# A graph network layer on one core: 32 instead of 24 columns an octet picked by TensorE, slightly fewer by ScalarE and VectorE, and the remainder table's operations in two places of VectorE's octet

## The chip, the core and the metric

The kernel runs on one core of a Trainium2 chip. The time is device microseconds of that core, the median of three runs. The profile and the trace come from one further execution on the same kind of core.

## The reference

A graph has 12,500 nodes with 64 features and 400,000 edges, sorted by their destination node. Each edge brings 16 features of its own. The layer makes a message for each edge, sums the messages of each node, and updates the nodes:

```python
m_in = jnp.concatenate([x[src], x[dst], edge_attr], axis=-1)
h = jax.nn.silu(m_in @ W1 + b1)
messages = jax.nn.silu(h @ W2 + b2)
agg = jax.ops.segment_sum(messages, dst, num_segments=x.shape[0])
node_in = jnp.concatenate([x, agg], axis=-1)
x = layernorm(x + jax.nn.silu(node_in @ W3 + b3))
```

Everything is float32. What is awkward is `x[src]`: the sources are random, so 400,000 rows of 256 bytes have to be fetched one by one.

## The kernel before, in words

**Tiles and octets.** 128 edges are a tile, and eight tiles are an octet, worked on as four pairs of tiles. There are 391 octets, and the main loop runs over them in order (`o`). Three octets make a chunk, for which the edge features are loaded together.

**Where a source row comes from.** A pair of tiles needs its 256 source rows. The kernel has five ways to get them, and they run side by side on different engines:

- POOL fetches a tile with one indirect DMA (L538, two for a pair) from `pa`, a table of `x @ W1[:64]` that the kernel writes to device memory in the first octets. Buffers for the fetched octets (`ga`) are five; POOL works three octets ahead.
- ScalarE (ACT) keeps `x` transposed in on-chip memory (`xs` in the lower half of the partitions, `x2` in the upper) and copies a column for each edge. One ACTIVATE with a column of `xs` as input and a column of `x2` as bias writes two edges (L447). 128 of them fill the table `cx` of one pair.
- VectorE (DVE) does the same with a maximum of two columns (L449).
- TensorE (PE) picks columns too: a matmul with a fixed matrix and one column of `xs` as moving operand puts the column into a PSUM bank. The first three tables (`EXACT`) are picked in float32 (L396). The later ones take two matmuls for a column, one with the upper 16 bits of `xs` (L400) and one with the remainder table `rest2` (L402). When a table is complete, DVE copies it out of PSUM in four pieces (`place`, L414) into `px`.
- SP fetches single rows with small direct DMAs (`rows`).

An octet's pairs that have a ready table (`slots`) or single rows (`rpairs`) are not gathered by POOL; the rest are. Tables are addressed by node numbers, which the engines read into registers first, 16 or 32 at a time; this is an instruction of the engine's own sequencer (L430 for DVE and ACT, L382 for PE).

**How the work is shared out.** `shares(eng, o)` says how many edges' columns an engine copies in octet `o`: for ACT 80 or 64, for DVE 64 or 96, by the ratio `VRATE`. `filled(o, b)` counts PE's picked columns of PSUM bank `b` ahead of octet `o`, 16 an octet for the exact tables and `PCOLS[1]` an octet after. `rcount` counts the single rows by the ratio `ROWS`. From these counts the lists `pairs`, `slots` and `rpairs` follow: a table is used two octets after it is full.

**One octet on each engine.** The order is written out by hand for PE, ACT, DVE and SP. Ahead of it, POOL runs freely until its `ga` buffers are all in use.

- PE: `turn(o + 1)` transposes the comparison of destinations (L605, into `ph`, one buffer), `window_product(o + 1)` (L562), `first_layer(o)` (L640 for gathered tiles, L643 for tables, L644 for destinations and edge features), the first half of the picks, `add_up(o - 4)` (L671), `second_layer(o - 2)` (L656, L658), the second half of the picks.
- ACT: a block of columns, SiLU of the first layer (`h`, L647), a block of columns, SiLU of the second (`m`, L662).
- DVE: `add_window` (L682), `place` if a table is complete, `compare_nodes(o + 2)` (`eh`, L587), two remainder operations in octets 9 to 58, a block of 16 column copies (for 32 edges), `window_copy(o + 1)` (L567), `turned(o + 1)` (`oh`, L615), a second block, and in some octets a third. Node updates are spread among these.

**The remainder table.** `remainders(k)` makes `rest2`, the part of `x` that the upper 16 bits leave out, 512 columns at a time in four steps: L810 for the lower half of the partitions, L812 (upper half, into spare space `left` of `v`), L814 (a copy of that to `rest2`), L816 (the difference of `left` and `rest2`). 25 blocks of columns make 100 steps. PE first reads `rest2` in octet 58.

Of the kernel before, what the change touches and what calls it, by code (L numbers as in the profile page):

```python
# [32 lines left out]
BEGIN = 4  # L33
PICK = 10
TABLES = 7
ACOLS = (48, 32)
VCOLS = (32, 0, 32, 32)
BASES = 16
PCOLS = (16, 24)
EXACT = 3  # L40
BATCH = 16
ROWS = (220, 13)
VRATE = (18, 7)
LOADS = (16, 32)
AADDR = 15616
RADDR = AADDR + 7360
# [16 lines left out]
def kernel(  # L63
# [51 lines left out]
    with ExitStack() as inner:  # L115
        flag = windows(inner, tc, ident, identb, twice, badi, pa, x, xt, xt2, src_c, src_row, src_pair, dst_c, dst_row, attr_t, attr_2, base, w1, b1, w2, b2, w3, b3, out, edges)
# [5 lines left out]
def windows(ctx, tc, ident, identb, twice, badi, pa, x, xt, xt2, src_c, src_row, src_pair, dst_c, dst_row, attr_t, attr_2, base, w1, b1, w2, b2, w3, b3, out, edges):  # L122
# [5 lines left out]
    NO = base.shape[1]  # L128
# [184 lines left out]
    with tc.tile_pool(name="gat", bufs=AHEAD + 2) as gat, \  # L313
# [20 lines left out]
        def shares(eng, o):  # L334
            if o < BEGIN:
                return (0, 0, 0, 0)
            if eng == ENG.Activation:
                return ACOLS if (o - BEGIN) % 7 % 3 < 2 else (ACOLS[0] - 16, ACOLS[1])
            n = (o + 1 - BEGIN) * VRATE[0] // VRATE[1] - (o - BEGIN) * VRATE[0] // VRATE[1]
            return VCOLS if n == 3 else VCOLS[:3] + (0,)  # L340


        def filled(o, b):
            first = range(PICK + (b - PICK) % 2, len(octs) + 8, 2)
            whole = EXACT * P // PCOLS[0]
            n = len(range(first.start, o, 2))
            return PCOLS[0] * min(n, whole) + PCOLS[1] * max(0, n - whole)

# [4 lines left out]
        for eng in (ENG.Activation, ENG.DVE):  # L353
            counts[eng] = [0]
            for o in range(len(octs) + 8):
                counts[eng].append(counts[eng][-1] + sum(shares(eng, o)))
# [59 lines left out]
        def columns(o, eng, part):  # L416
            if o < BEGIN:
                return
            lo = counts[eng][o] + sum(shares(eng, o)[:part])
            hi, most = lo + shares(eng, o)[part], LOADS[eng == ENG.DVE]  # L420
            while lo < hi:
                j, e0 = lo // (2 * P), lo % (2 * P)
                if j >= len(pairs[eng]):
                    return
                n = min(hi - lo, 2 * P - e0, most)
                key = eng, pairs[eng][j]
                if key not in cols:
                    cols[key] = cx.tile([P, P], F32, name="cx")
                t = cols[key].bitcast(U8)
                _, regs = nc.values_load_multi_w_load_instructions(  # L430
                    indices[eng, j][0:1, e0:e0 + n], engines=(eng,), min_val=XADDR,
                    max_val=X2ADDR + 4 * (N - 1), skip_runtime_bounds_check_because="src names a node")

                def at(i, u, a):
                    return u[:, ds(regs[i].with_bounds(min_val=a, max_val=a + 4 * (N - 1)) - a, 4)]

                def word(i, u, a):
                    o = (regs[i] - a).with_bounds(min_val=0, max_val=4 * (N - 1), guaranteed_mod_val=0, out_of_modulus=4)
                    return u[:, ds(o, 4)].bitcast(F32)

                for i in range(n):
                    e = e0 + i
                    if e % 8 >= 4:
                        continue
                    k = e // 8 * 4 + e % 4
                    if eng == ENG.Activation:
                        nc.scalar.activation(cols[key][:, k:k + 1], word(i, xb, XADDR), AF.Identity, bias=word(i + 4, x2b, X2ADDR))  # L447
                    else:
                        nc.vector.tensor_tensor(t[:, 4 * k:4 * k + 4], at(i, xb, XADDR), at(i + 4, x2b, X2ADDR), op=OP.max)  # L449
                lo += n  # L450
# [4 lines left out]
        def rcount(o):  # L455
            return max(0, o - RAW) * ROWS[0] // ROWS[1]

# [102 lines left out]
        def window_product(o):  # L560
            pw = mis.tile([P, P], F32, name="mm")
            nc.tensor.matmul(pw[:E, :], winrow[o], w1bb.rearrange("k s m -> k (s m)"),  # L562
                             start=True, stop=True)
            winrow[o] = pw

        def window_copy(o):
            nc.vector.tensor_tensor(xw[o % 3][:E, :], winrow.pop(o)[:E, :], mask[:E, :], op=OP.mult)  # L567
# [11 lines left out]
        def compare_nodes(o):  # L579
            c, t0, n, first, last = octs[o]  # L580
            eh = ehp.tile([P, OT // 2, S, 2], F32, name="eh")
            rel = dcs[t0 // SCT].bitcast(F32)
            t0 = t0 % SCT

            def compare(i, k, s, w):
                at = t0 + 2 * i + s
                nc.vector.tensor_tensor(eh[:, i:i + k, :, s:s + w], row[:, None, :, None].to_broadcast([P, k, S, w]),  # L587
                                        rel[:, at:at + k * w].rearrange("p (i s) -> p i s", s=w)[:, :, None, :].to_broadcast([P, k, S, w]),
                                        op=OP.is_equal)

            k = n // 2
            compare(0, k, 0, 2)
            if n % 2:
                compare(k, 1, 0, 1)
                nc.vector.memset(eh[:, k, :, 1], 0.0)
            hots[o] = [eh]
# [12 lines left out]
        def turned(o):  # L609
            c, t0, n, first, last = octs[o]  # L610
            eh, ph = hots[o]
            e = o % 3 * OT // 2 * P
            w = (n + n % 2) // 2 * P
            oh = loaded[c][:, e:e + w]
            nc.vector.tensor_copy(oh[:E, :], ph[:E, :(n + 1) // 2].rearrange("p i e -> p (i e)"))  # L615
            hots[o] = oh, eh
# [155 lines left out]
        for q in range(rest):  # L772
            o = lead[due[q]] + LAST - 1
# [11 lines left out]
        for q0, q1 in batches:  # L785
            o = lead[due[q1 - 1]] + LAST + 2 * G
# [10 lines left out]
        def remainders(k):  # L797

            c = k // 4 * RW
            if c >= N:  # L800
                return
            w = min(RW, N - c)
            at = slice(c, c + w)

            def top(t):
                return t.bitcast(BF16).rearrange("p (n s) -> p n s", s=2)[:, at, 1]

            left = v[D:, 2 * RB - 2:].rearrange("p a i d -> p (a i d)")[:, :w]
            if k % 4 == 0:
                nc.vector.tensor_tensor(rest2[:D, at], xs[:D, at], top(xs)[:D], op=OP.subtract)  # L810
            elif k % 4 == 1:
                nc.vector.tensor_tensor(left, x2[D:, at], top(x2)[D:], op=OP.subtract)  # L812
            elif k % 4 == 2:
                nc.vector.tensor_copy(rest2[D:, at], left)  # L814
            else:
                nc.vector.tensor_tensor(rest2[D:, at], left, rest2[D:, at], op=OP.subtract)  # L816
# [52 lines left out]
        with tc.manual_schedule(engines={ENG.PE, ENG.Activation, ENG.DVE, ENG.SP}):  # L869
# [8 lines left out]
            for o in range(NO + 2):  # L878
# [50 lines left out]
                        nc.vector.memset(t[:, c:min(c + XC, w)], 0.0)  # L929
                if o + 2 < NO:  # L930
                    compare_nodes(o + 2)
                for k in (2 * (o - BEGIN - 5), 2 * (o - BEGIN - 5) + 1) if o >= BEGIN + 5 else ():
                    remainders(k)
                columns(o, ENG.DVE, 0)
                def behind():
                    for q in adds.get(o, []):
# [18 lines left out]
                if o + 1 < NO:  # L955
                    if o + 1 < NO - 1:
                        window_copy(o + 1)
                    if o + 1 == NO - 2:
                        window_product(o + 2)
                        window_copy(o + 2)  # L960
                    columns(o, ENG.DVE, 1)
                    turned(o + 1)
                    columns(o, ENG.DVE, 2)
                columns(o, ENG.DVE, 3)
                if phase == 20:
# [62 lines left out]
def general(ctx, tc, ident, x, xt, src_c, dst_c, dst_row, attr_t, w1, b1, w2, b2, w3, b3, out, edges):  # L1028
# [9 lines left out]
    assert turns * U * P == edges  # L1038
    ROWS = N + P

# [3 lines left out]
    pb = dram.tile([N, D], F32, name="gpb")  # L1044
    accs = [dram.tile([ROWS, D], F32, name=f"acc{k}") for k in range(NACC)]

# [34 lines left out]
    with tc.tile_pool(name="gpre", bufs=3) as pre, tc.tile_pool(name="zero", bufs=1) as zp, \  # L1081
            tc.tile_pool(name="gpre_ps", bufs=4, space=PSUM) as pps:
        width = ROWS * D // P
        assert width * P == ROWS * D
        zero = zp.tile([P, width], F32, name="zero")
# [197 lines left out]
```

## Time and profile before

| what | value |
|---|---|
| median of three runs | 3247.89 us (3245.48 to 3252.06) |
| the profiled execution's own time | 3249.99 us |
| its span, first to last instruction | 3248.0 us |
| mean granted TensorE clock | 0.783 |
| PE busy (matmul) | 2642.2 us, 81% |
| DVE busy | 2119.8 us, 65% |
| ACT busy | 3084.4 us, 95% |
| POOL busy | 2425.1 us, 75% |
| indirect gathers by POOL (L538) | 2459 from `pa`, 84 from `x` |
| column copies by ACT (L447) and DVE (L449) | 14336 and 15616 |
| picks by PE of two matmuls (L400, L402) | 7680 |

A busy share is an average over the run; the octets before 58 differ from those behind it, as PE's picks and the remainder steps do. Idle time marked "issue" is time in which the engine waited for nothing that the profile shows; register loads of its own sequencer are among it.

### The profile page before, as it was taken

How to read it: one execution, taken by the hardware profiler on the slowest of the kernel's cores; microseconds unless marked ns; L12 is line 12 of the kernel's file. 1: busy time of each engine (PE TensorE's matmuls, PEld its weight loads, DVE VectorE, ACT ScalarE, POOL GpSimd, SP SyncE). 2: the span in 40 equal slices, each digit the busy share in tenths (PEclk: the TensorE clock that was granted, in tenths of full speed). 3: DMA queues.
4: the chain of work that ended last, by engine and by line, in shares of the span. 5: the costliest groups of instructions: out<-in, count | busy, mean ns of one | idle time of the engine just before them, and what ended most of it. 6: DMA issues, size and time to landing. Idle time of an engine off the chain costs nothing. (4 is left out here: it accounts for less than half of the span.)

```text
span 3248.0 us, 124643 instructions
## 1 busy us (share of the span) xinstructions
PE 2642.2 (81%) x32267; PEld 2170.6 (67%) x32267; DVE 2119.8 (65%) x18208; ACT 3084.4 (95%) x15185; POOL 2425.1 (75%) x2551
## 2 busy tenths in 40 slices
PE   7788778788787887887888888878888778888776
PEld 5677667676676766666666667667666666666664
DVE  5577777666666666666666666666666666666663
ACT  2799988999999999999999999999999999999994
POOL 7777776777777777777777777777777777777775
PEclk8787877787777777878877777877778788777887
DMA  7211111221221221222221222222221221222211
GB/s 148 49 41 40 40 39 37 43 48 42 43 43 41 49 43 43 43 46 44 43 44 41 46 43 43 43 43 46 43 44 41 45 46 42 44 43 45 44 41 36
DMA packets 157997, 148.42 MB, mean 46 GB/s; under 512 B 101606, under 2 KB 111604, under 8 KB 156516
## 3 DMA queue, kind: packets, MB, share of 16 engines
q0 software_dynamic: 81376, 83.49, 13.5%
q1 hardware_dynamic: 61406, 47.11, 5.6%
q10 hardware_dynamic: 14502, 9.75, 1.4%
q8 instruction: 272, 4.46, 0.6%
q14 instruction: 441, 3.61, 0.4%
HBM read 133.72 MB, written 6.40 MB: 43 GB/s over the span
## 5 line engine op out<-in xcount | busy, mean ns | idle before, releaser
L538 POOL DMA_INDIRECT ga<-pa,sc x2459 | 2344.6, 953 | 772.0 <-issue 661.0
L447 ACT ACTIVATE cx<-xs,x 128x1 f32 x14336 | 2829.6, 412 | 18.8 <-issue 14.8
L449 DVE TENSOR_TENSOR cx<-xs,x 128x4 uint8 x15616 | 1261.1, 155 | 1009.4 <-issue 989.8
L658 PEld LDWEIGHTS p<-w2d,h 128*128 128x128 f32 x3126 | 512.7, 233 | 245.9 <-issue 227.9
L402 PEld LDWEIGHTS <-twice 128*128 128x128 bf16 x7680 | 434.8, 100 | 265.5 <-issue 257.2
L400 PEld LDWEIGHTS <-twice 128*128 128x128 bf16 x7680 | 469.6, 100 | 124.6 <-issue 124.6
L644 PE MATMUL p<-oh,xw 128*128 128x512 f32 x760 | 545.9, 811 | 0.0
L400 PE MATMUL pg<-xs,twice 128*128 x7680 | 478.5, 165 | 69.5 <-DVE px L414 35.6
L658 PE MATMUL p<-w2d,h 128*128 128x128 f32 x3126 | 514.5, 319 | 0.0
L402 PE MATMUL pg<-rest,twice 128*128 x7680 | 468.0, 164 | 1.6 <-DVE rest L816 1.6
L605 PE MATMUL ph<-identb,eh 128*96 128x128 bf16 x1563 | 206.6, 271 | 243.2 <-DVE oh L615 237.2
L656 PE MATMUL p<-b2r,one 128*128 128x512 bf16 x391 | 172.6, 441 | 232.3 <-ACT m L662 231.3
L605 PEld LDWEIGHTS <-eh 128*96 128x96 bf16 x1563 | 150.5, 159 | 264.2 <-DVE oh L615 256.1
L647 ACT ACTIVATE h<-p 128x512 f32<-128x512 f32 x391 | 275.4, 704 | 52.6 <-PE p L644 27.1
L662 ACT ACTIVATE m<-p 128x512 f32<-128x512 f32 x391 | 276.0, 706 | 36.7 <-PE p L658 33.5
L671 PE MATMUL pg<-eh,m 128*64 128x48 f32 x6250 | 307.2, 245 | 0.7 <-ACT m L662 0.7
L640 PE MATMUL p<-ident,ga 128*128 128x128 f32 x1230 | 268.5, 344 | 10.6 <-DMA ga<-pa,sc 10.6
L671 PEld LDWEIGHTS pg<-eh,m 128*64 128x64 f32 x6250 | 255.7, 158 | 22.7 <-issue 13.3
L615 DVE COPY oh<-ph 96x512 f32<-96x512 f32 x391 | 263.3, 673 | 2.2 <-PE ph L605 2.1
L587 DVE TENSOR_TENSOR eh<-wrow,dc 128x384 f32<-128x384 f32 x392 | 213.3, 544 | 10.7 <-ACT z L726 6.1
L562 PE MATMUL mm<-w1bb,xr 66*96 66x128 f32 x782 | 214.8, 367 | 0.8 <-ACT rest L232 0.7
L640 PEld LDWEIGHTS p<-ident,ga 128*128 128x128 f32 x1230 | 206.1, 184 | 12.1 <-issue 12.1
(127 smaller groups left out, 1846.8 us busy)
## 6 DMA issues: line engine op xcount, KB each, us to landing
rx<-pa SPq DMA_DIRECT2D x6144, 0.2 KB
ga<-pa,sc POOLq DMA_INDIRECT x2459
oh<-in_attr SPq DMA_DIRECT2D x130, 192.0 KB
xr<-in_xt SPq DMA_DIRECT2D x391, 24.4 KB
cxi<-in_src_pair SPq DMA_DIRECT2D x234, 1.0 KB
xs<-in_xt ACTq DMA_DIRECT2D x6, 512.0 KB
pa<-rest ACTq DMA_DIRECT2D x12, 256.0 KB
x<-in_xt ACTq DMA_DIRECT2D x6, 512.0 KB
```

What stands on the lines that cost most here:

```text
L400: nc.tensor.matmul(g[:, s, k:k + 1], twice, xs.bitcast(U8)[:, ds(top, 2)].bitcast(BF16), start=True, stop=False, skip_group_check=True)
L402: nc.tensor.matmul(g[:, s, k:k + 1], twice, rest2.bitcast(U8)[:, ds(at, 2)].bitcast(BF16), start=False, stop=True, skip_group_check=True)
L447: nc.scalar.activation(cols[key][:, k:k + 1], word(i, xb, XADDR), AF.Identity, bias=word(i + 4, x2b, X2ADDR))
L449: nc.vector.tensor_tensor(t[:, 4 * k:4 * k + 4], at(i, xb, XADDR), at(i + 4, x2b, X2ADDR), op=OP.max)
L538: nc.gpsimd.indirect_dma_start(out=ga[:, i, :], out_offset=None, in_=x if o < RAW else pa[:, :], in_offset=bass.IndirectOffsetOnAxis(ap=sc ...
L605: nc.tensor.matmul(ph[:E, i, :], eh[:, i, :, 1], identb, start=(i == 0), stop=(i == k - 1), skip_group_check=True)
L640: nc.tensor.matmul(p1[:, i, :], g2.rearrange("p s d -> p (s d)"), ident, is_transpose=True, start=(i == c), stop=False, skip_group_check=True)
L644: nc.tensor.matmul(p1[:, :k], xw[o % 3], oh, start=False, stop=True, skip_group_check=True)
L647: nc.scalar.activation(h[:, :k], p1[:, :k], AF.Silu)
L658: nc.tensor.matmul(p2[:, 2 * i:2 * i + 2, :].rearrange("p s d -> p (s d)"), h[:, i, :], w2d, start=False, stop=(i == k - 1), skip_group_ch ...
L662: nc.scalar.activation(m[:, :n2], p2[:, :n2], AF.Silu)
L671: nc.tensor.matmul(pg[s * D:(s + 1) * D, :], m[:, i, :], eh[:, i // 2, :, s], start=(i < 2), stop=(i >= n - 2), skip_group_check=True)
```

## The change

`PCOLS[1]` goes from 24 to 32, so from octet 58 on PE picks 32 columns an octet. ACT takes 80 columns in two octets of three instead of five of seven, on average 74.7 instead of 75.4. DVE takes 81.6 on average instead of 82.3. Single rows go from 16.9 to 16.8 an octet. The two remainder steps of an octet, which stood together ahead of the first block of column copies, begin one octet earlier, and the second of them now stands behind `turned(o + 1)`, ahead of the second block.

```diff
 ACOLS = (48, 32)
 VCOLS = (32, 0, 32, 32)
 BASES = 16
-PCOLS = (16, 24)
+PCOLS = (16, 32)
 EXACT = 3
 BATCH = 16
-ROWS = (220, 13)
-VRATE = (18, 7)
+ROWS = (84, 5)
+VRATE = (51, 20)
...
             if eng == ENG.Activation:
-                return ACOLS if (o - BEGIN) % 7 % 3 < 2 else (ACOLS[0] - 16, ACOLS[1])
+                return ACOLS if (o - BEGIN) % 3 < 2 else (ACOLS[0] - 16, ACOLS[1])
...
                 if o + 2 < NO:
                     compare_nodes(o + 2)
-                for k in (2 * (o - BEGIN - 5), 2 * (o - BEGIN - 5) + 1) if o >= BEGIN + 5 else ():
-                    remainders(k)
+                spread = 2 * (o - BEGIN - 4) if BEGIN + 4 <= o < NO else None
+                if spread is not None:
+                    remainders(spread)
                 columns(o, ENG.DVE, 0)
...
                     columns(o, ENG.DVE, 1)
                     turned(o + 1)
+                    if spread is not None:
+                        remainders(spread + 1)
                     columns(o, ENG.DVE, 2)
```

## The prediction

> **What bounds the kernel now.** I read the table of stretches first, whole engines side by side, to see which engine is full in which part of the run (a stretch, its length, then busy time and instructions of PE, PEld, DVE, ACT and POOL, and the granted clock).
>
> ```profile
> span 3248.0 us, 124643 instructions
> ...
> core 0: us, PE busy (x) PEld busy (x) DVE busy (x) ACT busy (x) POOL busy (x), PEclk, DMA share, GB/s
> 250.00:560.00 310.00, 257.74 (x2477) 212.97 (x2475) 222.80 (x1706) 281.61 (x1385) 221.74 (x229) 0.80 0.19 39
> 700.00:3100.00 2400.00, 1972.46 (x25931) 1628.84 (x25930) 1579.39 (x14145) 2399.65 (x11913) 1817.04 (x1911) 0.78 0.20 44
> ```
>
> ACT is full from 700 us on. POOL looks only three quarters full, so I went to its timeline, and to what it waited for, first in 250 to 560 us, then in 700 to 3000 us.
>
> ```profile
> 1175.34 0.94 POOL L538 DMA_INDIRECT ga<-pa,sc  x1 [0.31 <-issue]
> 1176.59 0.95 POOL L538 DMA_INDIRECT ga<-pa,sc  x1 [0.30 <-issue]
> ...
> POOL ga L538 <- PE p L640: 19.5, 9, 4.9
> POOL ga L538 <- PE p L643: 2.3, 1, 2.3
> ...
> POOL ga L538 <- PE p L640: 5.8, 19, 0.3
> ...
> 3224.59 0.95 POOL L538 DMA_INDIRECT ga<-pa,sc  x1 [0.31 <-issue]
> ```
>
> A gather starts every 1.25 us: 0.95 busy and 0.30 of issue that belongs to it. 1911 of them in 2400 us are 1911 x 1.25 = 2388.8 us: POOL is full there too, and none of its waits on another engine exceeds that 0.30. In 250 to 560 us, 229 gathers are 286.3 us of 310, so 23.7 us are lost, and the waits for PE's L640 and L643 (a gather buffer that PE has not yet read) name 21.8 us of it, in ten waits that each contain the usual 0.30: 18.8 us. POOL issues its last gather at 3224.59 us, and 23 us of tail follow. So the end is set by the number of gathers times 1.25 us, plus what POOL loses in the early stage.
>
> Why PE is late in that stage: waits of ACT and PE in the same 250 to 560 us, then DVE's timeline over two octets.
>
> ```profile
> ACT m L662 <- PE p L658: 13.1, 7, 2.5
> ACT h L647 <- PE p L644: 6.7, 6, 2.1
> PE ph L605 <- DVE oh L615: 50.7, 20, 5.3
> ...
> 359.00 0.54 DVE L587 TENSOR_TENSOR eh<-wrow,dc 128x384 f32<-128x384 f32 x1
> 359.47 0.67 DVE L810 TENSOR_TENSOR rest<-xs 64x512 bf16<-64x512 f32 x1
> 360.17 0.73 DVE L812 TENSOR_TENSOR v<-x 64x512 f32<-64x512 f32 x1
> ...
> 363.83 1.32 DVE L449 TENSOR_TENSOR cx<-xs,x 128x4 uint8 x16 [0.83 <-issue]
> ...
> 367.92 0.55 DVE L587 TENSOR_TENSOR eh<-wrow,dc 128x384 f32<-128x384 f32 x1
> 368.49 0.42 DVE L814 CAST rest<-v 64x512 bf16<-64x512 f32 x1
> 368.95 0.72 DVE L816 TENSOR_TENSOR rest<-v,rest 64x512 bf16<-64x512 f32 x1
> 371.16 1.29 DVE L449 TENSOR_TENSOR cx<-xs,x 128x4 uint8 x16 [1.49 <-issue]
> ...
> 373.96 1.29 DVE L449 TENSOR_TENSOR cx<-xs,x 128x4 uint8 x16 [0.71 <-issue]
> ...
> 375.96 0.54 DVE L587 TENSOR_TENSOR eh<-wrow,dc 128x384 f32<-128x384 f32 x1
> ```
>
> DVE waits for nobody, PE waits for DVE's L615, ACT for PE, POOL for PE's L640: DVE sets this stage, at (375.96 - 359.00) / 2 = 8.48 us an octet here, and the idle pieces ahead of L449 are its 32-register loads.
>
> **The change part by part.**
>
> *Fewer gathers.* Following the constants through the functions shares, filled and rcount gives ACT 112 tables before and 111 after, DVE 122 and 121, PE 33 and 44, single rows 24 and 24. Nine more pairs of tiles come ready-made, so 18 gathers fall away (2543 to 2525), two more up to octet 75 and twenty fewer behind it. 18 x 1.25 = 22.5 us off POOL. The gain is only real if ACT and DVE keep POOL's pace.
>
> *ACT.* One table less is 128 instructions.
>
> ```profile
> 1703.39 4.82 ACT L447 ACTIVATE cx<-xs,x 128x1 f32 x24
> 1707.84 0.85 ACT L647 ACTIVATE h<-p 128x512 f32<-128x512 f32 x1
> ...
> 700.00:3100.00 2400.00, 201.36 (x299) 0.78 0.20 44
> ```
>
> (The second row is DVE's L615 alone: stretch, length, busy time and count.) 24 column copies of ACT take 1707.84 - 1703.39 = 4.45 us, 0.185 each, so 23.7 us fall away, 0.07 us an octet. 299 octets (by DVE's L615) pass in 2400 us, 8.03 each; ACT, with no wait of its own, goes to 7.96. POOL goes from 6.45 to 6.39 gathers an octet (tables counted over octets 69 to 367), 8.06 to 7.99 us. ACT stays just ahead.
>
> *DVE from octet 58 on.* 128 copies and their 8 loads go: a block of 16 occupies about 1.2 us plus 0.7 to 1.5 of load, 15 to 22 us in all. Eleven more PE tables bring 44 copies and 11 address operations (one ACT and one DVE address operation go). From the rows below the four copies of a table take 1.0 us from start to L587, and they lengthen the cover of the next load, so half is hidden: 11 x 0.5 to 1.0, with 3 us for addresses 8 to 14 us. DVE comes out between 14 us lighter and 1 us heavier; I take 9 lighter, 0.03 us an octet: about 8.00 us, level with POOL.
>
> ```profile
> 1175.44 0.93 DVE L414 COPY px<-pg 64x64 f32<-64x64 f32 x4
> 1176.41 0.56 DVE L587 TENSOR_TENSOR eh<-wrow,dc 128x384 f32<-128x384 f32 x1
> ```
>
> The Trainium skill ("SBUF — State Buffer", section "SBUF: two separate sides") states that some DVE operations lock a port pair against GpSimd, so that descriptors of POOL's DMAs wait for their end. Were that so for L414, 44 x 0.22 = 9.7 us would come onto POOL and the sum would be 3215. The trace disagrees: the gathers at 1175.34 and 1176.59, around four such copies, keep 1.25 us.
>
> *The moved operation, octets 8 to 57.* L810/L814 stay ahead of the first column block; L812/L816 go behind L615, ahead of the second. No DMA moves.
>
> ```profile
> L430 DVEq TENSOR_LOAD <-cxi x976: 2095/2100/2790, 64.5 to 3173.7; - x196
> ...
> 1712.71 1.28 DVE L449 TENSOR_TENSOR cx<-xs,x 128x4 uint8 x16 [0.64 <-issue]
> ```
>
> A load takes 2.10 us and runs under what DVE still has queued; without table operations 0.64 us stay open behind L587. In the octet with L810 and L812 both hide it and the second is mostly surplus, while 0.83 stays open behind L615. After the move each covers one load: of 0.70 + 0.76 + 0.83 = 2.29 us remain 0.70 + 0.05 + 0.76 + 0.14 = 1.65, 0.64 saved. In the octet with L814 and L816 the latter reads what the former has just written, and the load is not hidden: 368.49 to 371.16 is 2.67 us, plus 0.71 behind L615. I read it so that the dependent wait held back the load. An octet half apart, that wait is long over: 0.46 + 0.26 + 0.72 + 0.06 = 1.50 of 3.38, 1.88 saved. The mean is 1.26 us an octet, so DVE goes below ACT's 281.61 / 35 = 8.05 (its busy time over the stage's 35 octets) and stops setting the stage. POOL then gets back 18.8 (its named waits) to 23.7 us (its count); the lower end of the term is 0, if ACT or PE holds it instead. I take 20. PE needs the table one octet earlier than it does now, and it is finished one octet earlier.
>
> *TensorE.* Eight more columns an octet, two matmuls each.
>
> ```profile
> 1702.98 0.17 PE L402 MATMUL pg<-rest,twice 128*128 x1
> 1703.57 0.17 PE L402 MATMUL pg<-rest,twice 128*128 x1
> ...
> 1709.23 0.66 PE L605 MATMUL ph<-identb,eh 128*96 128x128 bf16 x4 [1.03 <-DVE oh L615]
> 1717.80 0.63 PE L605 MATMUL ph<-identb,eh 128*96 128x128 bf16 x4
> 1725.03 0.39 PE L605 MATMUL ph<-identb,eh 128*96 128x128 bf16 x4
> 1729.92 0.40 PE L605 MATMUL ph<-identb,eh 128*96 128x128 bf16 x4
> ...
> PE p L656 <- ACT m L662: 197.9, 139, 4.0
> PE ph L605 <- DVE oh L615: 145.6, 92, 4.3
> PE pg L400 <- DVE px L414: 29.9, 17, 4.5
> ...
> 1698.10:1721.90 23.80, 22.06 (x205) 17.53 (x205) 15.50 (x140) 23.80 (x122) 18.01 (x20) 0.50 0.19 41
> ```
>
> Twenty-two starts in 0.59 us are 0.027 each: 16 x 0.027 = 0.43 us an octet, 141 us over 327 octets. What hides it is PE's waiting (the three waits stand for 700 to 3000 us): 373 us of 2300, 1.30 us an octet. I cost it at nothing; without cover it is 141. The cover is uneven: at clock 0.50 an octet takes 8.57 us, more than the 8.03 allowed, at 1.00 it takes 4.89. After the change 9.00 and 5.32. In the half-clock stretch of 23.8 us PE falls back 2.9 us instead of 1.6.
>
> The Trainium skill ("TensorE: Matmul & The Clock Gate", "What's actually happening") has the full clock return after one busy window of about 3.4 us; then the added work would call it back sooner, and the term were 0 for certain. The row of 1698.10 shows half clock with PE 93% busy for 23.8 us, so here busy is not enough, and lateness is a rival.
>
> *Sum* against the profiled execution's own 3249.99 us (span 3248.0, 2 around it): 3249.99 - 22.5 - 20 + 0 = 3207.5. It lies 2.1 above the median shown, 3247.89, so the median becomes 3205.
>
> **The rivals.**
>
> *TensorE becomes the bound (slower).* The place is octets 58 to 385: more single-column matmuls stream less per window, the clock stays low. It decides when PE's mean octet passes 8.12 us (the 43 us gained, over 327 octets, on 7.99). With a share f of the time at full clock, f/5.32 + (1 - f)/9.00 = 1/8.12 gives f = 0.16, a mean clock of 0.58. At 0.55 the octet is 8.42 us, 0.43 x 327 = 141 us over: 3346. For it: the stretch above. Against: the clock is 0.78 now, and a late PE has no waits that thin its windows.
>
> *The early stage stays held* by ACT or PE, and only the gathers count: 3247.89 - 22.5 = 3225. For it: the ten waits name PE, not DVE. Against: PE itself waits 50.7 us on DVE there.
>
> *ACT or DVE fall behind POOL after octet 58*, through PE's lateness or the copies: 0.03 to 0.1 us an octet over 327 octets takes 10 to 33 us back, 3215 to 3238, with 3227 in the middle. For it: margins of 0.03 us for ACT and none for DVE. Against: ACT shows no wait on PE after 700 us.
>
> *It does not do what it says*: picked tables come late at L414 and hand back what the gathers gave, no change, 3247.
>
> **How the numbers follow.** Forecast 0.60 (own range 3197 to 3214: stalls 18.8 to 23.7, DVE's bounds, a few us of PE). Early stage held 0.15, falling behind 0.12, TensorE the bound 0.05, no change 0.04, more than forecast (POOL's other small gaps too) 0.04. The range 3197 to 3232 leaves out TensorE, no change, the better case and the upper end of falling behind, 0.17. Faster by over 0.2% (about what a measurement of this kernel can tell from no change) is 0.60 + 0.15 + 0.11 + 0.04 = 0.90; same 0.05, slower 0.05.
>
> **What would show it.** 2525 gathers at 1.25 us, the last near 3180 us. In 250 to 560 us POOL's waits on L640 below 5 us, and some 245 gathers. Blocks behind L816 without 1.49 us idle ahead of them. ACT full after 700 us, and no waits of ACT on PE. PE's wait of 1.30 us an octet down to some 0.9, clock at 0.75 or above. I am wrong if POOL waits on PE after 700 us, if ACT waits on L658 or L644 there, or if the clock falls below 0.65.

## The result, and the profile after

The changed kernel takes 3207.24 us (median of five runs, 3202.03 to 3208.39) against 3247.86 us of the kernel before (five runs, 3243.02 to 3252.06): a ratio of 0.9876, 95% interval 0.9862 to 0.9889. The forecast was 3205 us. The profiled execution took 3206.2 us.

The first view is again the table of stretches (length, busy time and instructions of PE, PEld, DVE, ACT and POOL, granted clock, share of the DMA engines).

```profile
span 3204.4 us, 137008 instructions
...
250.00:560.00 310.00, 260.92 (x2884) 217.93 (x2884) 239.26 (x1854) 308.27 (x1539) 235.86 (x244) 0.87 0.20 41
...
700.00:3000.00 2300.00, 1969.67 (x29471) 1606.26 (x29469) 1518.11 (x13530) 2285.87 (x11315) 1740.60 (x1834) 0.82 0.21 44
```

POOL's timeline, its last gather (start, duration and, in brackets, the idle time ahead of it):

```profile
3183.96 0.94 POOL L538 DMA_INDIRECT ga<-pa,sc  x1 [0.30 <-issue]
```

The last gather starts at 3183.96 us instead of 3224.59, 40.6 us earlier. In 250 to 560 us POOL now issues 244 gathers instead of 229, and 15 x 1.25 us is 18.8 us. The 18 gathers that fell away are 22.5 us. Together that is 41.3 us, the whole of the shift. The remaining 3 us of the span lie behind the last gather (20.4 us to the end instead of 23.4); as the medians differ by 40.6 us, these 3 us may be chance between two single executions.

DVE in the early stage of the changed kernel, over two octets:

```profile
350.62 0.54 DVE L587 TENSOR_TENSOR eh<-wrow,dc 128x384 f32<-128x384 f32 x1
351.08 0.68 DVE L810 TENSOR_TENSOR rest<-xs 64x512 bf16<-64x512 f32 x1
352.51 1.29 DVE L449 TENSOR_TENSOR cx<-xs,x 128x4 uint8 x16 [0.75 <-issue]
...
354.63 0.69 DVE L812 TENSOR_TENSOR v<-x 64x512 f32<-64x512 f32 x1
355.37 1.30 DVE L449 TENSOR_TENSOR cx<-xs,x 128x4 uint8 x16
...
360.68 0.42 DVE L814 CAST rest<-v 64x512 bf16<-64x512 f32 x1
361.57 1.27 DVE L449 TENSOR_TENSOR cx<-xs,x 128x4 uint8 x16 [0.47 <-issue]
...
363.68 0.69 DVE L816 TENSOR_TENSOR rest<-v,rest 64x512 bf16<-64x512 f32 x1
364.42 1.49 DVE L449 TENSOR_TENSOR cx<-xs,x 128x4 uint8 x16
```

Behind L812 and L816 no idle time is left ahead of the copies; ahead of the first block some remains. The waits that bear on the forecast's steps (total us, how many, the longest), in 250 to 560 us (the first three lines) and in 700 to 3000 us:

```profile
POOL ga L538 <- PE p L640: 0.9, 3, 0.3
ACT m L662 <- PE p L658: 1.1, 1, 1.1
PE ph L605 <- DVE oh L615: 28.1, 17, 3.2
...
ACT m L662 <- PE p L658: 1.5, 2, 0.8
ACT h L647 <- PE p L644: 1.4, 4, 0.6
PE pg L400 <- issue: 113.0, 280, 0.9
PE ph L605 <- DVE oh L615: 96.3, 71, 4.5
PE p L640 <- DMA ga<-pa,sc: 61.1, 63, 2.4
PE pg L400 <- DVE px L414: 31.1, 15, 4.1
PE p L656 <- ACT m L662: 24.0, 30, 2.1
```

POOL's waits for PE are gone from the early stage. Later, PE waits 61.1 us for gathered rows to land, which it did not do before: everything behind POOL has caught up with it.

### The profile page after: what moved, and what is told of

Same layout as the page of the kernel before. It is cut to its first block, busy times and chain, and to the rows that moved or that the text cites. A ratio compares the mean times of both kernels' runs of the same rounds, so it can differ in the third digit from the quotient of the medians.

```text
span 3204.4 us, 137008 instructions
## 1 busy us (share of the span) xinstructions
PE 2705.4 (84%) x37908; PEld 2208.7 (69%) x37908; DVE 2122.9 (66%) x18133; ACT 3060.4 (96%) x15057; POOL 2408.1 (75%) x2533
## 5 line engine op out<-in xcount | busy, mean ns | idle before, releaser
L447 ACT ACTIVATE cx<-xs,x 128x1 f32 x14208 | 2749.7, 338 | 19.7 <-issue 16.0
L402 PEld LDWEIGHTS <-twice 128*128 128x128 bf16 x10496 | 572.5, 99 | 399.0 <-issue 393.3
L400 PE MATMUL pg<-xs,twice 128*128 x10496 | 617.8, 164 | 168.1 <-issue 130.8
L400 PEld LDWEIGHTS <-twice 128*128 128x128 bf16 x10496 | 611.0, 99 | 114.8 <-issue 114.8
L402 PE MATMUL pg<-rest,twice 128*128 x10496 | 610.4, 164 | 0.0
L658 PEld LDWEIGHTS p<-w2d,h 128*128 128x128 f32 x3126 | 512.8, 233 | 86.0 <-issue 68.1
L658 PE MATMUL p<-w2d,h 128*128 128x128 f32 x3126 | 511.9, 318 | 0.0
L644 PE MATMUL p<-oh,xw 128*128 128x512 f32 x760 | 507.3, 757 | 0.0
L640 PE MATMUL p<-ident,ga 128*128 128x128 f32 x1221 | 255.9, 319 | 72.7 <-DMA ga<-pa,sc 71.8
L605 PE MATMUL ph<-identb,eh 128*96 128x128 bf16 x1563 | 185.2, 250 | 138.7 <-DVE oh L615 132.7
L647 ACT ACTIVATE h<-p 128x512 f32<-128x512 f32 x391 | 247.2, 632 | 40.2 <-PE p L635 19.2
L662 ACT ACTIVATE m<-p 128x512 f32<-128x512 f32 x391 | 247.3, 632 | 27.0 <-PE p L658 24.3
L615 DVE COPY oh<-ph 96x512 f32<-96x512 f32 x391 | 263.3, 673 | 2.2 <-PE ph L605 2.1
L640 PEld LDWEIGHTS p<-ident,ga 128*128 128x128 f32 x1221 | 182.8, 166 | 91.9 <-issue 74.0
L605 PEld LDWEIGHTS <-eh 128*96 128x96 bf16 x1563 | 136.1, 145 | 154.0 <-DVE oh L615 146.8
L656 PE MATMUL p<-b2r,one 128*128 128x512 bf16 x391 | 174.7, 447 | 70.3 <-ACT m L662 69.4
L562 PE MATMUL mm<-w1bb,xr 66*96 66x128 f32 x782 | 191.6, 333 | 0.8 <-ACT rest L232 0.7
```

The costliest lines, as they stand in the source:

```text
L400: nc.tensor.matmul(g[:, s, k:k + 1], twice, xs.bitcast(U8)[:, ds(top, 2)].bitcast(BF16), start=True, stop=False, skip_group_check=True)
L402: nc.tensor.matmul(g[:, s, k:k + 1], twice, rest2.bitcast(U8)[:, ds(at, 2)].bitcast(BF16), start=False, stop=True, skip_group_check=True)
L605: nc.tensor.matmul(ph[:E, i, :], eh[:, i, :, 1], identb, start=(i == 0), stop=(i == k - 1), skip_group_check=True)
L640: nc.tensor.matmul(p1[:, i, :], g2.rearrange("p s d -> p (s d)"), ident, is_transpose=True, start=(i == c), stop=False, skip_group_check=True)
L644: nc.tensor.matmul(p1[:, :k], xw[o % 3], oh, start=False, stop=True, skip_group_check=True)
L658: nc.tensor.matmul(p2[:, 2 * i:2 * i + 2, :].rearrange("p s d -> p (s d)"), h[:, i, :], w2d, start=False, stop=(i == k - 1), skip_group_ch ...
```

## The experiments

Ratios are to the kernel before, run on the same chip beside it. In each expectation theory A and theory B are two accounts that the run is to tell apart.

### Four kernels on a slower chip

Four kernels ran first: the move alone, the shares alone, the remainder steps reordered, and repeated picks.

The move alone keeps the new place of the second step and the old constants:

```diff
-PCOLS = (16, 32)
-ROWS = (84, 5)
-VRATE = (51, 20)
+PCOLS = (16, 24)
+ROWS = (220, 13)
+VRATE = (18, 7)
...
-                return ACOLS if (o - BEGIN) % 3 < 2 else (ACOLS[0] - 16, ACOLS[1])
+                return ACOLS if (o - BEGIN) % 7 % 3 < 2 else (ACOLS[0] - 16, ACOLS[1])
```

> The kernel before with the moved remainder step alone (shares as before, 2543 gathers). Theory A (the two parts add: the move gives back only what POOL loses in the early stage, the shares only the 18 gathers): 3229 us (3225 to 3233), POOL's waits on L640 in 250 to 560 us below 3 us, last gather some 18 us earlier than before. Theory B (the move is worth nothing alone, because ACT at its old share is level with POOL and hands the gain back after octet 58): 3240 us or more, with the early waits gone but POOL waiting on L640 after 700 us.

The shares alone are the new constants in the kernel before, the reverse of that diff on top of it.

> The kernel before with the new shares alone (2525 gathers, the two remainder steps together as before). Theory A (parts add): 3225 us (3221 to 3229); POOL's waits on L640 and L643 in 250 to 560 us stay near 20 us. Theory B (the lighter shares of ACT and DVE free the early stage too): 3212 us or less, and those waits below 8 us.

The reordered steps, in the kernel before:

```diff
-                for k in (2 * (o - BEGIN - 5), 2 * (o - BEGIN - 5) + 1) if o >= BEGIN + 5 else ():
+                b = (o - BEGIN - 5) // 2
+                for k in (((1,) if o == BEGIN + 4 else ()) if o < BEGIN + 5 else
+                          (4 * b + 2, 4 * b) if (o - BEGIN - 5) % 2 == 0 else (4 * b + 3, 4 * b + 5)):
                     remainders(k)
```

> The kernel before, with both remainder steps of an octet still together ahead of the first block of copies, but L814 paired with L810 and L816 with the next block's L812, so that no step reads what the step just ahead of it wrote. Theory A (the dependent wait of L816 on L814 holds back the register load, and it is most of the gain of the move): the 1.49 us idle ahead of L449 in every second octet is gone, and the time is near that of the move alone, 3230 us (3226 to 3236). Theory B (the gain is that each step covers one load, so the places matter): at most a third of it, 3241 us or more.

And four picks of each half octet made twice, in the kernel before:

```diff
-                for i in range(n):
+                for i in [*range(n), *(range(min(n, 4)) if j >= EXACT else ())]:
                     s, k = (e0 + i) % 8 // 4, (e0 + i) // 8 * 4 + i % 4
```

> The kernel before, with the first four picks of every half octet from octet 58 on made twice (the same columns into the same places, result unchanged): TensorE gets the added 16 matmuls an octet, nobody is relieved, only the 4 more columns of a register load are missing. Theory A (the added matmuls lie in PE's waits): 3248 us within 4, PE's waits shorter by some 0.4 us an octet. Theory B (they come late at ACT and DVE): between 3255 us and 3248 + 141 = 3389 us, with ACT waiting on L644 or L658.

On the chip of these runs the kernel before takes 5251.94 us, not 3248. The move alone has a ratio of 1.0002 (0.9993 to 1.0012), the shares alone 1.0908 (1.0889 to 1.0926), the reordered steps 0.9998 (0.9988 to 1.0008), the repeated picks 1.0881 (1.0863 to 1.0899). The move alone, there: first the chain that ended last, by engine.

```profile
PE 62%; issue 32%; ACT 1%; DVE 1%; another core or an unknown queue 0%; ACTq 0%; DVEq 0%
```

Its waits in 1000 to 2000 us (total, how many, the longest):

```profile
PE p L658 <- issue: 300.8, 347, 1.8
POOL ga L538 <- PE p L640: 413.1, 74, 6.7
```

And PE's timeline:

```profile
2703.90 0.56 PE L658 MATMUL p<-w2d,h 128*128 128x128 f32 x1 [0.87 <-issue]
2705.35 0.37 PE L658 MATMUL p<-w2d,h 128*128 128x128 f32 x1 [0.88 <-issue]
2706.81 0.37 PE L658 MATMUL p<-w2d,h 128*128 128x128 f32 x1 [1.09 <-issue]
2708.94 0.37 PE L658 MATMUL p<-w2d,h 128*128 128x128 f32 x1 [1.75 <-issue]
```

Here PE is the bound from end to end, and it stands idle between matmuls that wait for nothing the profile shows. So DVE's order is worth nothing, and every added pick is paid: the shares alone add 2816 picks of two matmuls (10496 instead of 7680) and 478.8 us, 0.170 us each; the repeated picks add 2720 and 462.7 us, 0.170 us each as well. The whole change was not run there; as its move is worth nothing and its shares cost 9%, it must be expected to be slower. On the stages of the forecast these runs say nothing. So the first three were run again on other chips; the repeated picks were not.

### The move alone

> The moved remainder step alone once more, since the first four runs came from a chip on which the kernel before takes 5252 us and PE's own issue sets the time (there it is worth nothing, as PE's front end is the bound throughout). On a chip where the kernel before takes some 3248 us: theory A (parts add) 3229 us (3225 to 3233), POOL's waits on L640 in 250 to 560 us below 3 us; theory B (worth nothing alone, ACT hands it back after octet 58) 3240 us or more. On a chip of the slow kind: 5252 us within 10 by both.

On a chip where the kernel before takes 3242.82 us: 3226.14 us, 0.9951 (0.9935 to 0.9968), 16.7 us less. Its row of the early stage, and POOL's wait there:

```profile
250.00:560.00 310.00, 257.72 (x2789) 213.46 (x2789) 239.03 (x1861) 308.21 (x1541) 235.87 (x244) 0.87 0.20 42
...
POOL ga L538 <- PE p L640: 0.3, 1, 0.3
```

244 gathers, as in the changed kernel. The gain of the early stage is the move's alone, and the old shares do not hand it back: theory A.

### The shares alone

> The new shares alone once more (2525 gathers, remainder steps together as before). On a chip where the kernel before takes some 3245 us, theory A (parts add): ratio 0.993, some 22 us less than before, 3222 us; POOL's waits on L640 and L643 in 250 to 560 us stay near 20 us, and TensorE's added picks show nowhere else. Theory B (the lighter shares free the early stage too): ratio 0.989 or less, those waits below 8 us. On a chip of the kind where the kernel before takes 5252 us: 1.09, TensorE's issue being the bound there.

3222.53 us against 3245.0: 0.9935 (0.9917 to 0.9952), 22.5 us less. POOL's wait in 250 to 560 us:

```profile
POOL ga L538 <- PE p L640: 19.3, 10, 5.1
```

It stays where it was. 18 x 1.25 is 22.5 us as well, though the interval reaches from 15.6 to 26.9 us; the eight more picks an octet cost nothing that shows. The stage has 232 gathers here, against 229 before and 244 with the whole change. 0.9951 x 0.9935 = 0.9886, inside the interval of the whole change: the parts add.

### What the wait between neighbours does

> The reordered remainder steps once more: both steps of an octet still together ahead of the first block of copies, but L814 paired with L810 and L816 with the next block's L812, so that no step reads what the step just ahead of it wrote. On a chip where the kernel before takes some 3245 us, theory A (the dependent wait held back the register load, and this is most of the move's gain): 0.995 to 0.996 of before, as with the move alone, the 1.49 us idle ahead of L449 gone from every second octet. Theory B (the places matter, each step covering one load): 0.998 or above. Where the kernel before takes 5252 us: no change by both.

3246.66 us against 3245.0: 1.0003 (0.9994 to 1.0013), no change. The timeline of the octet with L816:

```profile
368.17 0.69 DVE L816 TENSOR_TENSOR rest<-v,rest 64x512 bf16<-64x512 f32 x1
368.89 0.69 DVE L812 TENSOR_TENSOR v<-x 64x512 f32<-64x512 f32 x1
371.10 1.27 DVE L449 TENSOR_TENSOR cx<-xs,x 128x4 uint8 x16 [1.52 <-issue]
```

POOL's wait in 250 to 560 us stays too:

```profile
POOL ga L538 <- PE p L640: 17.3, 10, 4.7
```

The edit had put one wait in another's place. L812 writes the scratch that L816, just ahead, still reads, so it waits as L816 had waited for L814, and 1.52 us stay idle. By the numbers that was theory B, but the test was not clean. The next kernel differs by a second scratch area, used by turns:

```diff
-            left = v[D:, 2 * RB - 2:].rearrange("p a i d -> p (a i d)")[:, :w]
+            left = v[D:, 2 * RB - 2 - k // 4 % 2 * 2:][:, :2].rearrange("p a i d -> p (a i d)")[:, :w]
```

> The kernel before, remainder steps still together ahead of the first block, paired as in the run before (L814 with L810, L816 with the next block's L812), and now with two scratch areas by turns, so that L812 no longer writes what L816 just ahead of it reads. In the run before, that wait stood where L816's own had stood and 1.6 us stayed idle ahead of L449. Theory A (a wait between neighbours holds the register load back, wherever the two stand): the idle is gone from every second octet, POOL's waits on L640 in 250 to 560 us below 5 us, and 0.995 to 0.996 of before. Theory B (the second place is what counts): idle behind L615 remains 0.8 us in every octet, ratio 0.998 or above, early waits of 15 us or more.

3223.78 us against 3242.86: 0.9942 (0.9925 to 0.9959), 19.1 us less. The same octet:

```profile
367.25 0.69 DVE L816 TENSOR_TENSOR rest<-v,rest 64x512 bf16<-64x512 f32 x1
367.86 0.68 DVE L812 TENSOR_TENSOR v<-x 64x512 f32<-64x512 f32 x1
368.57 1.29 DVE L449 TENSOR_TENSOR cx<-xs,x 128x4 uint8 x16
...
371.39 1.33 DVE L449 TENSOR_TENSOR cx<-xs,x 128x4 uint8 x16 [0.74 <-issue]
```

And POOL's wait in 250 to 560 us:

```profile
POOL ga L538 <- PE p L640: 1.2, 4, 0.3
```

The register load for the block behind the two steps can be seen itself. Its duration in ns and its start in the kernel before, with the reordered steps, and with two scratch areas:

```profile
L430 DVEq TENSOR_LOAD <-cxi x1: 2103/2103/2103, 369.0 to 369.0; - x1
L430 DVEq TENSOR_LOAD <-cxi x1: 2103/2103/2103, 368.9 to 368.9; - x1
L430 DVEq TENSOR_LOAD <-cxi x1: 2097/2097/2097, 366.1 to 366.1; - x1
```

In the first two the load starts only when the second, waiting step does (L816 at 368.95, L812 at 368.89). In the third it starts 1.1 us ahead of the first step, and is over at 368.2, before the copies begin at 368.57.

Both steps stand together in the old place, 0.74 us stay idle behind L615, and the time is that of the move. What held the early stage was the wait between neighbours; the second place is one way to get rid of it, and a second scratch area is another. Theory A.

### Is POOL the only bound after the change?

In nine octets the changed kernel leaves out the last pair's two gathers, and TensorE reads the third pair's rows instead. That saves 18 gathers that no engine takes over.

```diff
+                if i // 2 == 3 and short(o):
+                    continue
                 nc.gpsimd.indirect_dma_start(
...
+                    f = 2 if i == 3 and short(o) else i
-                    g2 = single.pop(o) if o in rpairs and i == c else ga[:, 2 * i:2 * i + 2, :]
+                    g2 = single.pop(o) if o in rpairs and i == c else ga[:, 2 * f:2 * f + 2, :]
```

> The changed kernel with 18 gathers less that nobody takes over: in nine octets between 70 and 380 the last pair is not fetched and TensorE reads the third pair's rows in its place (so the source rows of these nine pairs are wrong). Theory A (POOL's count times 1.25 us is still the only bound after the change): 22.5 us less than the changed kernel, a ratio of 0.981 to the kernel before instead of 0.988. Theory B (ACT and DVE are level with POOL by now): half of that or less, 0.984 or above, with POOL waiting on L640 or ACT on nothing at all up to the end.

3185.06 us against 3242.86: 0.9816 (0.98 to 0.9833). The changed kernel's 0.9876 less this is 0.0060, 19.5 us, for 22.5 us of gathers. The row of 700 to 3100 us (this file's lines stand eight lower):

```profile
700.00:3100.00 2400.00, 2044.24 (x30918) 1689.33 (x30917) 1588.94 (x14175) 2394.44 (x11869) 1816.59 (x1914) 0.83 0.19 44
```

And what ACT waits for in 700 to 3000 us:

```profile
ACT cx L447 <- issue: 3.2, 7, 0.6
```

Theory A: after the change POOL's count still sets the end. ACT is busy for 2394.44 of 2400 us, so there is little room behind it.

### How far TensorE's cover reaches

```diff
-PCOLS = (16, 32)
+PCOLS = (16, 40)
```

> The changed kernel with 40 instead of 32 columns an octet (54 instead of 44 tables of TensorE, 2505 gathers instead of 2525), ACT and DVE as in the changed kernel. Theory A (POOL's count is the bound, TensorE has room for 0.43 us more): up to 25 us less than the changed kernel, 0.980 to 0.983 of the kernel before. Theory B (TensorE's cover is used up, its lateness reaches ACT): 0.987 or more, with ACT's waits on L644 and L658 after 700 us above 20 us.

and, with the first twelve picks of each half octet made twice in the changed kernel (the edit of the repeated picks, with 12 for 4):

> The changed kernel with the first twelve picks of every half octet from octet 58 on made twice (the result is unchanged, nobody is relieved): 48 more matmuls an octet, 48 x 0.027 = 1.30 us, against 1.13 us an octet that TensorE still waits in 700 to 3000 us of the changed kernel (325 us of 2300). Theory A (that wait is the whole cover): 3207 + 0.17 x 327 = 3262 us or more, ratio 1.004 or more, ACT waiting on L644 and L658. Theory B (the granted clock rises with the load and makes room): 3207 to 3220 us, ratio below 0.992, clock above 0.82.

These two ran on another of the slower chips, where the kernel before takes 5135.52 us: 1.1426 (1.1393 to 1.1458) and 1.2020 (1.1994 to 1.2047). PE and its issue make up 97 to 98% of the chain that ended last in both, so neither tells the theories apart. The last run repeats the first of them on a chip where the kernel before takes 3245 us; the second was not run again:

> The changed kernel with 40 instead of 32 columns an octet once more (2505 gathers instead of 2525). On a chip where the kernel before takes some 3245 us, theory A (POOL's count is the bound, TensorE has room for 0.43 us more): 0.980 to 0.983 of the kernel before. Theory B (TensorE's cover is used up, its lateness reaches ACT): 0.987 or more, with ACT's waits on L644 and L658 after 700 us above 20 us. On a chip where the kernel before takes over 5000 us, TensorE's issue being the bound: 1.14.

3267.33 us against 3244.95: 1.0081 (1.0053 to 1.0109). Its row of 700 to 3000 us:

```profile
700.00:3000.00 2300.00, 2104.05 (x33045) 1737.98 (x33040) 1482.18 (x13166) 2234.39 (x10989) 1689.79 (x1779) 0.79 0.21 43
```

And the waits of that time:

```profile
POOL ga L538 <- PE p L640: 80.7, 55, 5.1
...
ACT m L662 <- PE p L658: 11.7, 28, 1.6
ACT h L647 <- PE p L644: 11.1, 15, 1.8
...
PE pg L400 <- issue: 84.5, 247, 0.9
```

Theory B: twenty gathers fewer, and POOL waits for PE 55 times. ACT is idle for 65.6 us of 2300, 22.8 of them in waits on PE, and PE is the bound, at a granted clock of 0.79: it waits for other engines for only 65.6 us as well (L605 37.3, L414 27.3, L656 1.0). TensorE's room ends between 32 and 40 columns. Of the versions that compute the layer, the changed kernel remains the fastest.

## Why the prediction was right, and where its working was off

*Fewer gathers*, 22.5 us: right. The shares alone give 22.5 us, and leaving out 18 more gives nearly as much again. That POOL, three quarters busy on the page, is full at 1.25 us a gather is what carried the forecast.

*The early stage*, 20 us (18.8 to 23.7): right in size and in mechanism. POOL gets 15 gathers more into 250 to 560 us, 18.8 us; the move alone is worth 16.7 us, the two scratch areas 19.1 us. The reason given, that a step waiting on its neighbour holds the next register load back, was shown by the pair of kernels that differ in the scratch area only, and by the starts of the load itself.

*DVE's saving an octet*, 1.26 us: too large. In the octet with L814 and L816 there remain 361.57 - 360.68 and 364.42 - 363.68, 0.89 + 0.74 = 1.63 us, where 1.50 were forecast. In the octet with L810 and L812 there remain 1.43 + 0.74 = 2.17 instead of 1.65, so that the move saved 0.12 there, not 0.64: one step alone does not hide the first load. It did no harm, because DVE only had to fall below ACT and POOL; ACT is busy for 308.27 of 310 us now.

*DVE from octet 58 on*: the sum has a slip. By its own terms (15 to 22 us go, 8 to 14 come) DVE comes out between 1 and 14 us lighter, not up to 1 us heavier. No run isolates this term.

*TensorE at no cost*: right for 32 columns, by a smaller margin than worked out. The waits on other engines that stood against the added work were to fall from 1.30 us an octet to about 0.9. L605, L640, L414 and L656 sum to 212.5 us of 2300, at 8.02 us an octet 0.74. The term left out is the issue of the picks. The waits ahead of L400 and the register loads of the picks (duration in ns: least, median, largest; first and last start), first in the kernel before, then in the changed one:

```profile
PE pg L400 <- issue: 31.0, 112, 0.5
L382 PEldq TENSOR_LOAD <-pxi x728: 328/848/1293, 144.1 to 3126.7; - x182
...
PE pg L400 <- issue: 113.0, 280, 0.9
L382 PEldq TENSOR_LOAD <-pxi x704: 1101/1105/1390, 144.2 to 3156.8; - x176
```

And two starts of an octet on PE in the changed kernel (its clock is 1.00 from 1703 to 1709 us), with the first pick of the second half:

```profile
1703.01 0.40 PE L605 MATMUL ph<-identb,eh 128*96 128x128 bf16 x4
1708.15 0.16 PE L400 MATMUL pg<-xs,twice 128*128 x1 [0.31 <-issue]
1708.95 0.40 PE L605 MATMUL ph<-identb,eh 128*96 128x128 bf16 x4
```

The wait ahead of L400 went from 31.0 to 113.0 us, 0.29 us an octet, while a register load went from 0.85 us (12 columns) to 1.10 us (16). Address arithmetic follows each load; ahead of the pick at 1708.15 the load runs from 1706.13 to 1707.24, and behind it come six such operations (`top` in the kernel; first and last start):

```profile
L389 PEldq FUSED_REGOPS  x6: 42/74/74, 1707.3 to 1708.1; - x6
```

The octet at full clock shown here takes 5.94 us instead of the 5.32 forecast. Together: of the 0.56 us by which the waits on other engines fell, 0.29 are issue and 0.27 are PE's busy time, which rose from 6.60 to 6.86 us (1972.46 us over 299 octets, 1969.67 over 287), at a clock that rose from 0.78 to 0.82; the forecast had 0.43 of busy time and no issue.

The rival in which TensorE becomes the bound was priced with octets of 5.32 and 9.00 us, and so decided only below a clock of 0.58. With 40 columns it came true at 0.79: the point from which it decides was badly placed. One can see it in the kernel before, where the same formula gives 6.03 us an octet (4.89 and 8.57 us, clock 0.78), while PE was busy for 6.60 and stood another 0.11 in issue ahead of L400. What the two octets chosen for it leave out is not shown. From 32 to 40 columns PE's busy time rose to 7.54 us an octet (2104.05 over 279), 0.25 more than the added picks' 0.43, while the issue ahead of L400 fell to 0.30. So issue took half of the room that the step to 32 used, and the matmuls took what the step to 40 used; whether their 0.25 us come from the lower clock (0.79 instead of 0.82) is not shown.

*ACT without waits on PE after 700 us*: nearly, 2.9 us. *Copies of L414 against POOL's gathers*: the shares alone lost nothing to them.

*Not foreseen*: 3 us behind the last gather in the one pair of profiled executions, a granted clock that rises (the forecast had only bounded it), and chips on which the shares cost 9%.

## What to carry to other kernels

An engine can be full at three quarters of its busy time: count its instructions in a stretch and multiply by the distance of two starts before you look for the bound elsewhere. An operation that waits on its neighbour costs more than its own wait if a register load stands behind it; give it another buffer or another operation in between. Work put onto an engine with idle time costs nothing only until that idle time is used up, and register loads and address arithmetic can use it up as matmuls do: price them all, and test the price on the kernel you already have.

## What the runs showed of the hardware

On two of the chips the same kernel before takes 5252 and 5136 us instead of 3243 to 3248. The trace of the move alone on the first of them shows PE idle for 0.87 to 1.75 us between matmuls of L658, put down to issue, while POOL, ACT and DVE wait for PE. An added pick of two matmuls costs 0.170 us there in both kernels that add them, though picks once begun follow each other every 0.027 us as on the other chips (2700.25 to 2700.84 us of the move alone, 22 starts). What slows PE's issue on these chips is not shown by any run and stays open.

The granted clock does not simply follow PE's busy time: with PE 93% busy it stayed at 0.50 for 23.8 us in the kernel before, and with a third more picks its mean over the run rose by 0.04. With 40 columns it fell back to 0.80.

A register load on VectorE takes 2.10 us for 32 registers. Behind an operation that waits for the one just ahead of it, it started only with that operation (369.0 us, L816 at 368.95), and the copies behind it came 2.2 us later. Without the wait it started 1.1 us ahead of both operations (366.1 us, L816 at 367.25), and the copies had no idle time ahead of them.
